# Values by seven products of half blocks, in turns with the keys, in an attention and graph convolution kernel

## The chip, the cores and the metric

The kernel runs on one core of a Trainium2 chip. Its time is the device time of one launch in microseconds (us); runs of one kernel on one chip are compared with runs of the other. In the profile, PE is TensorE, PEld its weight loads, DVE is VectorE, ACT is ScalarE, POOL is GpSimd, SP is the engine that issues the transfers. L405 is line 405 of the kernel.

## What is computed

The input is x, 16 batches of 1024 nodes with 256 channels, in fp32. Cut to what matters here, the first layer is

```python
fea  = transpose(x, (0, 2, 1))
Wg   = adj * likeness(mean of x over channels)      # per batch, 1024 x 1024
q    = relu((fea @ Wg) * para)                      # split in 4 heads of 64
kv   = x @ kv_w                                     # kv_w is 256 x 512
k, v = first 256 columns, last 256 columns          # keys and values, 4 heads each
out  = softmax(q k^T * scale) v
x    = layernorm(x + out)
```

The second layer is two graph convolutions with a residual and a layernorm:

```python
h = relu(x @ w1_loop + adj @ (x @ w1_neigh) + b1)
h = relu(h @ w2_loop + adj @ (h @ w2_neigh) + b2)
x = layernorm(x + (x + h) * 0.5)
```

The change concerns `v`, the values: per batch a product of x (1024 x 256) with the right half of `kv_w` (256 x 256).

## The kernel before

All 16 batches go through one long program whose order is written out by hand (`tc.manual_schedule()`): each engine does its instructions in the order in which the program names them, and waits where a tile isn't ready or its buffer isn't free. Work of several batches is woven together. While batch b is in its attention, the queries, keys and values of batch b + 1 are prepared, and the convolutions of batches b - 1 and b - 2 are done.

Attention of a batch has four units (two pairs of heads by two halves of the queries). A unit is `scores` (L594, TensorE, with the exponentials on ScalarE at L597 and their running sum on VectorE at L601 and L603) and then `outputs` (L614). After the fourth unit come the last products of the queries for the next batch (`FastQueries.step`, L546), then the keys and values of the next batch (`KeysValues.run`), and then the next batch's first scores, which need both.

Several products are already done by a scheme with seven products of half blocks in place of eight: the matrices are cut in 2 x 2 blocks, sums of blocks are made beforehand, and seven products are added up in a fixed pattern. The queries are done so (`FastQueries`, 28 products per batch, added by `end`, L555 to L563), the products with `adj` of the convolutions (`Joined`), and the keys (`KeysValues`). In `KeysValues`:

- `sums` makes the four sums of the blocks of x on VectorE; `self.w[n]` is the right factor of product n, [128 channels, 512 nodes].
- `sum_key_weights` makes the four sums of the key weights once, on GpSimd, and leaves them in DRAM; `load` brings them back for each batch (512 columns of a tile of 1024); `self.a[n]` is the left factor of product n, [128, 128].
- `run` does the products 1, 2, 6, 5, 7, 4, 3. Three products are added in PSUM onto an earlier one (`again=True`), after ScalarE has copied the earlier state out. Three PSUM tiles are used: 1, 6, 5 and 3 go to `first`; 2 to `third`; 7 and 4 to `second`.
- Between the keys' products stand four groups of the values. `value_group` (L355 to L362) makes two node tiles of 128 with all 256 channels: four products of 256 columns, with the tiles of x as weights.

A product of the program is two matmul instructions in the profile.

PSUM is shared out by two tags: `big`, three tiles of [128, 1024], and `bank`, two tiles of [128, 512]. `half_psum` takes a whole `big` tile and uses half of it. The tiles of a tag are handed out as they come free, and a tile is free when its last reader is done. The queries' products hold all three `big` tiles (products 1 and 6 in the first, 2 and 7 in the second, 5 and 3 in the third) and one `bank` tile (product 4) until `FastQueries.end` has added them up. Its adds read the first tile last at L556, the second at L558, the `bank` tile at L559 and the third at L563. Between L559 and L561 `end` calls `norm.sum_squares`, which sums the squares of the batch in normalization on VectorE (L319, L254).

`run` takes two callbacks. `between` is `norm.variance`: `fold_sums` (L247 to L251), one small product on TensorE that adds the sums of squares over the partitions, into a `bank` tile, and then the reciprocal deviation (L324 on VectorE, L326, a power, on GpSimd). `later` is `q.scale` (L569, L570), which finishes the queries. The part of the main loop that calls all this for batches 2 to 15:

```python
qT = q.end(norm.sum_squares)
xB = load_blocked(b + 1, f"a{b + 1}")
load_next()
kT, v = kv.run(norm.variance, q.scale)
...
norm.scale()
norm.spread()
```

Batches 0 and 1 use the plain functions `keys` and `values`.

Of the kernel before, what the change touches and what calls it, by code (L numbers as in the profile page):

```python
# [10 lines left out]
F32 = mybir.dt.float32  # L11
# [7 lines left out]
def kernel(  # L19
# [31 lines left out]
    nc = tc.nc  # L51

    B, N, C = x.shape
    P = 128
    NT = N // P
    NC = C // P
# [3 lines left out]
    FB = 512  # L60
    NJ = N // FB
    TJ = FB // P
    EPS = 1e-5
# [19 lines left out]
    dram = ctx.enter_context(tc.tile_pool(name="dram", bufs=2, space=bass.MemoryType.DRAM))  # L83

    def big_psum(name):
        return psum.tile([P, N], F32, tag="big", name=name, bufs=3)

    def half_psum(name):
        return big_psum(name)[:, 0:FB]

    def bank_psum(name):
        return psum.tile([P, FB], F32, tag="bank", name=name, bufs=2)
# [6 lines left out]
    def row_tile(name):  # L99
        return work.tile([P, N], F32, tag="row", name=name, bufs=ROWS)  # L100
# [15 lines left out]
    for t0 in range(0, NT, 2):  # L116
        nc.sync.dma_start(out=x_first[:, t0:t0 + 2, :],
                          in_=x[0, t0 * P:(t0 + 2) * P, :].rearrange("(t p) c -> p t c", p=P))
    kvw_sb = const.tile([P, NC, 2 * C], F32, name="kvw_sb")
# [6 lines left out]
    b2_sb = const.tile([P, C], F32, name="b2_sb")  # L126


    key_sums = dram.tile([P, 4 * P], F32, tag="key_sums", name="key_sums", bufs=1)

    def sum_key_weights():
        a11, a21, a12, a22 = (kvw_sb[:, cc, ts(kb, P)] for cc in range(NC) for kb in range(NC))
        t = row_tile("key_sums")
        s1, s2, s3, s4 = (t[:, ts(n, P)] for n in range(4))
        nc.gpsimd.tensor_add(s1, a21, a22)
        nc.gpsimd.tensor_sub(s2, s1, a11)
        nc.gpsimd.tensor_sub(s3, a11, a21)
        nc.gpsimd.tensor_sub(s4, a12, s2)
        nc.sync.dma_start(out=key_sums, in_=t[:, 0:4 * P])

    def load_weights():
        nc.sync.dma_start(out=w1l_sb, in_=w1_loop.rearrange("(cc p) f -> p cc f", p=P))
# [79 lines left out]
    def prepare_first(xb):  # L222

        xT = work.tile([P, NC, N], F32, tag="xT", name="xT_0", bufs=2)
        c_col = small.tile([P, NT], F32, tag="c_col", name="c_col_0", bufs=2)
        pts = [[half_psum(f"xT_ps_0_{cc}") for cc in range(NC)], [bank_psum(f"xT_ps_1_{cc}") for cc in range(NC)]]
        for j in range(NJ):
            for t in range(j * TJ, (j + 1) * TJ):
                for cc in range(NC):
                    nc.tensor.transpose(pts[j][cc][:, ts(t - j * TJ, P)], xb[:, t, ts(cc, P)], ident)  # L230
            for cc in range(NC):
                (nc.vector.tensor_copy if cc else nc.scalar.copy)(xT[:, cc, ts(j, FB)], pts[j][cc])
        for j in range(NJ):
            rows = slice(j * TJ, (j + 1) * TJ)
            nc.vector.tensor_reduce(c_col[:, rows], xb[:, rows, :], AX.X, ALU.add)
        nc.vector.tensor_scalar_mul(c_col, c_col, 1.0 / C)
        return xT, c_col
# [6 lines left out]
        nc.scalar.copy(c_row, pc)  # L244
        return c_row

    def fold_sums(part, name):  # L247

        pm = bank_psum(f"{name}_ps")
        nc.tensor.matmul(pm[:, 0:NB], fold.rearrange("p a k -> p (a k)"), part[:, 0, :], start=True, stop=True)  # L250
        return pm[:, 0:NB]  # L251

    def join(part):
        nc.vector.tensor_add(part[:, 0, :], part[:, 0, :], part[:, 1, :])  # L254
# [40 lines left out]
    def by_node(t):  # L295
        return t.rearrange("p (bn r) -> p bn r", r=S)

    class BlockedNorm:
# [22 lines left out]

        def variance(self):
            self.rstd = small.tile([P, NB], F32, tag="rstd1", name=f"rstd1_{self.name}", bufs=2)
            nc.vector.tensor_scalar(self.rstd, fold_sums(self.part, f"sum2_{self.name}"), 1.0 / C, EPS,  # L324
                                    op0=ALU.mult, op1=ALU.add)
            nc.gpsimd.tensor_tensor(self.rstd, self.rstd, neg_half, ALU.pow)  # L326

# [27 lines left out]
    def value_group(b, v, xT, g, copy):  # L355
        per = FB // C
        pv = bank_psum(f"v_ps_{b}_{g}")
        for i in range(per):
            for cc in range(NC):
                nc.tensor.matmul(pv[:, ts(i, C)], xT[:, cc, ts(g * per + i, P)], kvw_sb[:, cc, C:2 * C],  # L360
                                 start=(cc == 0), stop=(cc == NC - 1))
        copy(v[:, g * per:(g + 1) * per, :], pv.rearrange("p (i c) -> p i c", c=C))  # L362
# [7 lines left out]
    class KeysValues:  # L370
# [17 lines left out]
            self.w = {1: w11, 2: w21, 3: w22, 4: t4, 5: t1, 6: t2, 7: t3}  # L388

        def load(self):  # L390
            t = row_tile(f"key_sums_{self.b}")
            nc.sync.dma_start(out=t[:, 0:4 * P], in_=key_sums)
            a11, a21, a12, a22 = (kvw_sb[:, cc, ts(kb, P)] for cc in range(NC) for kb in range(NC))
            self.a = {1: a11, 2: a12, 3: t[:, ts(3, P)], 4: a22, 5: t[:, ts(0, P)], 6: t[:, ts(1, P)], 7: t[:, ts(2, P)]}

        def run(self, between, later):
            b, xT = self.b, self.xT
            kT = work.tile([P, NC, N], F32, tag="kT", name=f"kT_{b}")
            v = work.tile([P, NT, C], F32, tag="v", name=f"v_{b}")
            first, third, second = (half_psum(f"k_ps_{b}_{i}") for i in range(3))  # L400
            s12, s34 = (row_tile(f"ksnap_{b}_{k}") for k in range(2))
            p1, u1, u3, p7 = s12[:, 0:FB], s12[:, FB:N], s34[:, 0:FB], s34[:, FB:N]

            def product(n, dst, again=False):
                nc.tensor.matmul(dst, self.a[n], self.w[n], start=not again, stop=True, skip_group_check=again)  # L405

            def group(g):
                value_group(b, v, xT, g, nc.scalar.copy)

            product(1, first)  # L410
            nc.scalar.copy(p1, first)
            product(2, third)
            group(0)
            product(6, first, again=True)
            nc.scalar.copy(u1, first)
            group(1)
            between()
            nc.vector.tensor_add(kT[:, 0, 0:FB], p1, third)
            product(5, first, again=True)
            nc.scalar.copy(u3, first)  # L420
            product(7, second)
            nc.scalar.copy(p7, second)
            group(2)
            later()
            product(4, second, again=True)
            nc.vector.tensor_add(kT[:, 1, 0:FB], u1, second)
            nc.gpsimd.tensor_add(kT[:, 1, FB:N], u3, p7)
            product(3, first, again=True)
            nc.scalar.copy(kT[:, 0, FB:N], first)
            group(3)  # L430
            return kT, v

    class Queries:
# [49 lines left out]
    class FastQueries(Queries):  # L483
# [16 lines left out]
        def block(self, i, j):  # L500
            return self.xb[:, j * TJ:(j + 1) * TJ, ts(i, P)]
# [70 lines left out]
    class Attention:  # L572
# [47 lines left out]
        def add(self, u):  # L620

            b, (pair, j) = self.b, UNITS[u]
            half = FB // S
            pd = bank_psum(f"den_ps_{b}_{u}")
            den = pd[:, 0:2 * half]
            nc.tensor.matmul(den, fold.rearrange("p a k -> p (a k)"), self.part.pop(u), start=True, stop=True)  # L626
            rden = self.rden[:, ts(u, half)]
            for s in range(2):
                rows = slice(s * HD, (s + 1) * HD)
                nc.vector.reciprocal(rden[rows, :], den[rows, ts(s, half)])  # L630
            o = by_node(self.o.pop(u))
            nc.vector.tensor_mul(o, o, rden.unsqueeze(2).to_broadcast([P, half, S]))
            dst = by_node(self.xB[pair][:, ts(j, FB)])
            nc.vector.tensor_add(dst, dst, o)
            nc.vector.tensor_reduce(self.sums[:, pair, ts(j, half)], dst, AX.X, ALU.add)
            if u == len(UNITS) - 1:
                join(self.sums)
                nc.vector.tensor_reduce(rden_min[:, b:b + 1], self.rden, AX.X, ALU.min)
                nc.vector.tensor_reduce(rden_max[:, b:b + 1], self.rden, AX.X, ALU.max)
# [274 lines left out]
    def run():  # L914
# [10 lines left out]
        xT, c_col = prepare_first(x_first)  # L925
        q = Queries(0, x_first)
        for t in range(NT):
            q.load(t)
        sum_key_weights()
        q.load_para()  # L930
        blocked = load_blocked(1, "1")
        tiles = {mt: adj_blocked(mt) for mt in (0, TJ, 1)}
# [6 lines left out]
        kT = keys(0, xT, first_weights)  # L939
        for t in (1, 2):  # L940
            q.likeness(t)
        v = values(0, xT, nc.vector.tensor_copy)
# [28 lines left out]
        for b in range(B):  # L971
# [87 lines left out]
            if more and not c1:  # L1059
                xT = ready["xT"]  # L1060
# [32 lines left out]
                kT, v = keys(b + 1, xT), values(b + 1, xT)  # L1093
            elif more:
# [11 lines left out]
                kT, v = kv.run(norm.variance, q.scale)  # L1106
# [33 lines left out]
    with tc.manual_schedule():  # L1140
        run()
# [14 lines left out]
    with tc.If(count < P):  # L1156
        with tc.For_i(0, B, 1) as b:
            xb = load_x(b, "z")
            xT = channel_major(load_blocked(b, "z"), "xT_z")
            q = Queries("z", xb)  # L1160
            means(q, xb, "z")()
            kT, v = keys("z", xT), values("z", xT)
# [46 lines left out]
```

## Time and profile before

| | |
|---|---|
| time, median of 3 runs | 2170.1 us (2170.02 to 2170.28) |
| span of the profiled run | 2168.3 us |
| granted TensorE clock, mean | 0.999 |
| busy: TensorE, VectorE, ScalarE, GpSimd | 2153.5, 1892.3, 1027.7, 367.2 us |
| values, L360, all batches, TensorE busy | 120.2 us |
| keys in `KeysValues`, L405, 196 instructions | 96.7 us |

The first lines are for the whole program; the busy time of an engine counts the time in which at least one of its instructions runs. The last two rows are the groups of instructions of those lines; the 96.7 is the sum of the four groups of L405 (41.8, 26.3, 14.3 and 14.3 us). Matmuls overlap one another, so the distance from one start to the next says what a product costs, and not the length of one record.

### The profile page before, as it was taken

How to read it: one execution, taken by the hardware profiler on the slowest of the kernel's cores; microseconds unless marked ns; L12 is line 12 of the kernel's file. 1: busy time of each engine (PE TensorE's matmuls, PEld its weight loads, DVE VectorE, ACT ScalarE, POOL GpSimd, SP SyncE). 2: the span in 40 equal slices, each digit the busy share in tenths (PEclk: the TensorE clock that was granted, in tenths of full speed). 3: DMA queues.
4: the chain of work that ended last, by engine and by line, in shares of the span. 5: the costliest groups of instructions: out<-in, count | busy, mean ns of one | idle time of the engine just before them, and what ended most of it. 6: DMA issues, size and time to landing. Idle time of an engine off the chain costs nothing.

```text
span 2168.3 us, 23079 instructions
## 1 busy us (share of the span) xinstructions
PE 2153.5 (99%) x8054; PEld 1024.9 (47%) x8054; DVE 1892.3 (87%) x2343; ACT 1027.7 (47%) x1346; POOL 367.2 (17%) x208
## 2 busy tenths in 40 slices
PE   9999999999999999999999999999999999999997
PEld 5344444444444444444544445454454444544354
DVE  5978998898998989988889888999989899898965
ACT  4744545545355453445444454445553445535411
POOL 1011130211303113030120302203022130211021
PEclk9999999999999999999999999999999999999999
DMA  9493663846557375573655536566384654744342
GB/s 230 117 136 117 139 158 101 143 130 117 147 127 161 102 127 154 128 171 89 115 165 124 160 88 116 171 122 156 97 123 154 122 155 115 131 137 83 117 138 97
DMA packets 611771, 286.22 MB, mean 132 GB/s; under 512 B 504768, under 2 KB 569152, under 8 KB 611648
## 3 DMA queue, kind: packets, MB, share of 16 engines
q1 hardware_dynamic: 611376, 284.15, 55.5%
q8 instruction: 65, 1.06, 0.2%
q14 instruction: 58, 0.48, 0.1%
q10 hardware_dynamic: 272, 0.52, 0.1%
HBM read 238.16 MB, written 46.46 MB: 131 GB/s over the span
## 4 chain that ended last, share of the span: by engine, by line
PE 97%; DVE 2%; ACT 0%; DMA 0%; issue 0%; SPq 0%; POOLq 0%; DVEq 0%; POOL 0%
PE s L594 20%; PE av L614 20%; PE hu_ps L873 17%; PE g_ps L546 16%; PE v_ps L360 5%; PE k_ps L405 4%; PE t_ps L712 3%; PE h_ps L780 3%; PE hu_ps L719 2%; PE g_ps L473 2%; PE h_ps L781 2%; DVE acc L603 1%; PE h_ps L734 1%; PE u_ps L763 1%; PE k_ps L350 1%; PE den_ps L626 0%
## 5 line engine op out<-in xcount | busy, mean ns | idle before, releaser
L597 ACT ACTIVATE pr<-s 128x1024 f32<-128x1024 f32 x512 | 476.1, 1052 | 176.6 <-PE s L594 176.6
L603 DVE TENSOR_TENSOR acc<-acc,pr 128x1024 f32<-128x1024 f32 x384 | 494.1, 1287 | 41.1 <-DVE acc L603 1.0
L594 PE MATMUL s<-qT,kT 64*128 64x512 f32 x2048 | 457.1, 596 | 0.7 <-ACT qT L480 0.7
L614 PE MATMUL av<-pr,v 128*64 128x512 f32 x2048 | 453.6, 595 | 0.0
L594 PEld LDWEIGHTS s<-qT,kT 64*128 64x128 f32 x2048 | 191.1, 185 | 236.1 <-ACT pr L597 114.1
L614 PEld LDWEIGHTS av<-pr,v 128*64 128x64 f32 x2048 | 141.4, 137 | 300.0 <-issue 285.7
L326 POOL TENSOR_TENSOR rstd<-rstd,neg_half 128x32 f32<-128x32 f32 x16 | 87.1, 5443 | 1111.5 <-DVE rstd L324 1111.5
L459 ACT ACTIVATE wg<-c_row,c_col 128x1024 f32<-128x1024 f32 x128 | 146.9, 1148 | 69.5 <-DVE accB L605 51.3
L465 DVE SCALAR_TENSOR_TENSOR wg<-wg,adj 128x1024 f32<-128x1024 f32 x128 | 149.8, 1209 | 11.3 <-ACT wg L460 10.4
L873 PE MATMUL hu_ps<-adj,R 128*128 128x512 f32 x360 | 158.3, 596 | 0.0
L460 ACT ACTIVATE wg<-wg 128x1024 f32<-128x1024 f32 x128 | 135.3, 1057 | 4.1
L314 ACT ACTIVATE sq<-xB_a 128x1024 f32<-128x1024 f32 x32 | 33.8, 1057 | 194.4 <-DVE xB_a L309 193.1
L360 PE MATMUL v_ps<-kvw_sb,xT 128*128 128x256 f32 x512 | 120.2, 379 | 0.1
L546 PE MATMUL g_ps<-wg,S 128*128 128x512 f32 x224 | 116.7, 603 | 0.0
L360 PEld LDWEIGHTS v_ps<-kvw_sb,xT 128*128 128x128 f32 x512 | 97.2, 190 | 38.4 <-issue 21.0
L546 PE MATMUL g_ps<-T,S 128*128 128x512 f32 x224 | 114.4, 592 | 0.0
L546 PE MATMUL g_ps<-wg,x 128*128 128x512 f32 x224 | 109.0, 599 | 0.0
L873 PE MATMUL hu_ps<-adjT,t 128*128 128x512 f32 x240 | 105.7, 592 | 0.0
L873 PEld LDWEIGHTS hu_ps<-adj,R 128*128 128x128 f32 x360 | 67.3, 190 | 78.9 <-issue 78.4
L601 DVE TENSOR_TENSOR acc<-pr,pr 128x1024 f32<-128x1024 f32 x64 | 76.8, 1200 | 23.7 <-ACT pr L597 23.7
L605 DVE STREAM_TRANSPOSE accB<-acc 128x1024 f32<-128x1024 f32 x64 | 79.7, 1245 | 3.2
L889 ACT COPY snap<-hu_ps 128x512 f32<-128x512 f32 x15 | 8.8, 586 | 150.2 <-PE hu_ps L873 150.2
(185 smaller groups left out, 2916.0 us busy)
## 6 DMA issues: line engine op xcount, KB each, us to landing
adj<-in_adj_dram SPq DMA_DIRECT2D x128, 512.0 KB, 4.5
adj<-adjT SPq DMA_DIRECT2D x120, 512.0 KB, 10.2
para<-in_L_gnn_para_dram SPq DMA_DIRECT2D x32, 512.0 KB, 3.3
xB_a<-in_x_dram SPq DMA_DIRECT2D x128, 128.0 KB, 4.2
x1d<-xB_a SPq DMA_DIRECT2D x128, 128.0 KB, 3.4
x<-x1d SPq DMA_DIRECT2D x16, 1024.0 KB, 15.4
xB<-in_x_dram SPq DMA_DIRECT2D x120, 128.0 KB, 4.5
x<-in_x_dram SPq DMA_DIRECT2D x15, 1024.0 KB, 7.0
```

The costliest lines, as they stand in the source:

```text
L326: nc.gpsimd.tensor_tensor(self.rstd, self.rstd, neg_half, ALU.pow)
L360: nc.tensor.matmul(pv[:, ts(i, C)], xT[:, cc, ts(g * per + i, P)], kvw_sb[:, cc, C:2 * C], start=(cc == 0), stop=(cc == NC - 1))
L405: nc.tensor.matmul(dst, self.a[n], self.w[n], start=not again, stop=True, skip_group_check=again)
L459: nc.scalar.activation(wg, self.c_row, AF.Abs, bias=self.c_col[:, t:t + 1], scale=-1.0)
L460: nc.scalar.activation(wg, wg, AF.Tanh, scale=-0.5)
L465: nc.vector.scalar_tensor_tensor(wg, wg, 1.0, self.adj.pop(t), op0=ALU.add, op1=ALU.mult)
L546: nc.tensor.matmul(self.p[n], x_n[:, k, :], w_n, start=(k == 0), stop=(k == TJ - 1))
L594: nc.tensor.matmul(ps[:, ts(s, FB)], self.kT[rows, pair, ts(mt, P)], self.qT[rows, pair, ts(j, FB)], start=True, stop=True)
L597: nc.scalar.activation(pr, ps, AF.Exp)
L603: nc.vector.tensor_add(acc, acc, pr)
L614: nc.tensor.matmul(pav[s * HD:(s + 1) * HD, :], self.v[:, mt, pair * P + s * HD:pair * P + (s + 1) * HD], self.pr[mt][:, ts(s, FB)], start ...
L873: nc.tensor.matmul(dst, self.x[n][:, k, :], half_adj[w][:, k, :] if w else of_rows(rows, k), start=(start and k == 0), stop=(k == TJ - 1), ...
```

## The change

The values are now computed by seven products of half blocks too. Their right factors are cut from the other half of `kv_w`, with sums made once at the start as for the keys (`sum_kv_weights`, now a full tile of 1024 columns); the sums of x are those of the keys, used here as weights. A value product n is four matmuls of 128 columns, one for each node tile of the half. Keys and values take turns: key n, value n, in the order 1, 2, 6, 7, 5, 4, 3. The purpose is less work on TensorE: 28 products of 128 columns in place of 16 of 256 columns.

The value products hold two `bank` tiles (`v_first` for products 1, 6, 5 and 3, `v_next` for 2 and then for 7 and 4). The fold of the variance therefore goes to a `big` tile. It stands after key 2 and value 2; before, it stood after key 2, group 0, key 6 and group 1.

```diff
-    def sum_key_weights():
+    def sum_kv_weights():
+        t = row_tile("kv_sums")
+        for k in range(2):
+            a11, a21, a12, a22 = (kvw_sb[:, cc, ts(2 * k + kb, P)] for cc in range(NC) for kb in range(NC))
+            s1, s2, s3, s4 = (t[:, ts(4 * k + n, P)] for n in range(4))
...
+        nc.sync.dma_start(out=kv_sums, in_=t)
...
-    def fold_sums(part, name):
+    def fold_sums(part, name, psum_tile=bank_psum):
-        pm = bank_psum(f"{name}_ps")
+        pm = psum_tile(f"{name}_ps")
...
-            nc.vector.tensor_scalar(self.rstd, fold_sums(self.part, f"sum2_{self.name}"), 1.0 / C, EPS,
+            nc.vector.tensor_scalar(self.rstd, fold_sums(self.part, f"sum2_{self.name}", half_psum), 1.0 / C, EPS,
...
+        def value(self, n, dst, again=False):
+            for t in range(TJ):
+                nc.tensor.matmul(dst[:, ts(t, P)], self.w[n][:, ts(t, P)], self.a[1][n],
+                                 start=not again and t == 0, stop=True, skip_group_check=again or t > 0)
...
-            product(1, first)
-            nc.scalar.copy(p1, first)
-            product(2, third)
-            group(0)
-            product(6, first, again=True)
-            nc.scalar.copy(u1, first)
-            group(1)
+            k_first, v_first = half_psum(f"k_ps_{b}_0"), bank_psum(f"v_ps_{b}_0")
+            self.key(1, k_first)
+            copy(p1, k_first)
+            self.value(1, v_first)
+            copy(y1, v_first)
+            k_next, v_next = half_psum(f"k_ps_{b}_1"), bank_psum(f"v_ps_{b}_1")
+            self.key(2, k_next)
+            self.value(2, v_next)
             between()
-            nc.vector.tensor_add(kT[:, 0, 0:FB], p1, third)
-            product(5, first, again=True)
-            nc.scalar.copy(u3, first)
-            product(7, second)
-            nc.scalar.copy(p7, second)
-            group(2)
+            add(kT[:, 0, 0:FB], p1, k_next)
+            add(block(0, 0), tiles(y1), tiles(v_next))
+            self.key(6, k_first, again=True)
+            copy(u1, k_first)
+            self.value(6, v_first, again=True)
+            copy(z1, v_first)
+            k_next, v_next = half_psum(f"k_ps_{b}_2"), bank_psum(f"v_ps_{b}_2")
+            self.key(7, k_next)
+            copy(p7, k_next)
+            self.value(7, v_next)
+            copy(y7, v_next)
+            self.key(5, k_first, again=True)
+            copy(u3, k_first)
+            self.value(5, v_first, again=True)
+            copy(z3, v_first)
             later()
-            product(4, second, again=True)
-            nc.vector.tensor_add(kT[:, 1, 0:FB], u1, second)
+            self.key(4, k_next, again=True)
+            add(kT[:, 1, 0:FB], u1, k_next)
             nc.gpsimd.tensor_add(kT[:, 1, FB:N], u3, p7)
-            product(3, first, again=True)
-            nc.scalar.copy(kT[:, 0, FB:N], first)
-            group(3)
+            self.value(4, v_next, again=True)
+            self.key(3, k_first, again=True)
+            copy(kT[:, 0, FB:N], k_first)
+            add(block(1, 0), tiles(z1), tiles(v_next))
+            self.value(3, v_first, again=True)
+            copy(block(0, 1), tiles(v_first))
+            nc.gpsimd.tensor_add(block(1, 1), tiles(z3), tiles(y7))
             return kT, v
```

`block(i, j)` is the half of the value tile with channels i and node tiles j; `y1`, `z1`, `z3` and `y7` are ScalarE's copies of the value products, in two more row tiles.

## The prediction

> **What bounds the kernel now.** I read the page first, then the groups of instructions with the shapes kept apart, then the waits of TensorE, and last the timeline of one batch's keys and values. Of the page, the first block gives busy time and share of the span of each engine, the second the engines' shares of the chain that ended last:
>
> ```profile
> PE 2153.5 (99%) x8054; PEld 1024.9 (47%) x8054; DVE 1892.3 (87%) x2343; ACT 1027.7 (47%) x1346; POOL 367.2 (17%) x208
> ...
> PE 97%; DVE 2%; ACT 0%; DMA 0%; issue 0%; SPq 0%; POOLq 0%; DVEq 0%; POOL 0%
> ```
>
> TensorE is the bound, and the list of its waits adds up to about 4 us over the whole span. So there is no slack on TensorE to hide anything in: a microsecond less of its work is a microsecond gained, and a microsecond in which it waits is one lost. VectorE at 87% is the engine to suspect for such waits.
>
> What a product costs comes from the groups by form. After the x stand the number of instructions, the busy time of the group, and the mean length of one; each product of the program is two instructions here:
>
> ```profile
> L360 PE MATMUL v_ps<-kvw_sb,xT 128*128 128x256 f32 x512 | 120.2, 379 | 0.1
> ...
> L712 PE MATMUL t_ps<-w1n_sb,x1T 128*128 128x128 f32 x512 | 61.3, 278 | 0.0
> ```
>
> The mean lengths overlap one another and are not what counts; the distance from start to start does. It can be read in the timeline (start, length, engine, line, operation, number of instructions merged) of batch 8's keys and values, which run while batch 7 is normalized:
>
> ```profile
> 1054.40 1.88 PE L405 MATMUL k_ps<-xT,kvw_sb 128*128 128x512 f32 x4
> 1056.12 1.89 PE L360 MATMUL v_ps<-kvw_sb,xT 128*128 128x256 f32 x8
> 1057.85 1.02 PE L405 MATMUL k_ps<-K,key_sums 128*128 128x512 f32 x2
> 1058.70 1.89 PE L360 MATMUL v_ps<-kvw_sb,xT 128*128 128x256 f32 x8
> 1060.43 0.30 PE L250 MATMUL sum_ps<-sq_part,fold 128*128 128x32 f32 x2
> 1060.57 1.96 PE L405 MATMUL k_ps<-K,key_sums 128*128 128x512 f32 x4
> ...
> 1067.63 7.14 PE L594 MATMUL s<-qT,kT 64*128 64x512 f32 x32
> ```
>
> and, from the same view of VectorE,
>
> ```profile
> 1053.22 0.69 DVE L556 TENSOR_TENSOR U<-P,g_ps 128x512 f32<-128x512 f32 x1 [1.66 <-ACT P L555]
> 1053.82 0.68 DVE L557 TENSOR_TENSOR qT<-P,g_ps 128x512 f32<-128x512 f32 x1
> 1054.42 0.68 DVE L558 TENSOR_TENSOR U<-U,g_ps 128x512 f32<-128x512 f32 x1
> 1055.20 0.69 DVE L559 TENSOR_TENSOR qT<-U,g_ps 128x512 f32<-128x512 f32 x1
> 1055.81 2.34 DVE L319 TENSOR_REDUCE sq_part<-sq 128x32 f32<-128x1024 f32 x2
> 1058.18 0.19 DVE L254 TENSOR_TENSOR sq_part<-sq_part 128x32 f32<-128x32 f32 x1
> 1058.29 0.68 DVE L561 TENSOR_TENSOR qT<-U,g_ps 128x512 f32<-128x512 f32 x1
> 1058.89 0.68 DVE L562 TENSOR_TENSOR U<-U,g_ps 128x512 f32<-128x512 f32 x1
> 1059.60 0.69 DVE L563 TENSOR_TENSOR qT<-U,g_ps 128x512 f32<-128x512 f32 x1
> ```
>
> Call the start of the first key product T0 (1054.40). The stage ends when the scores start, T0 + 13.23. A key product takes (1056.12 - 1054.40)/2 = 0.86 us, a value group of four products of 256 columns 1.73, the fold (L250, the sum over channels of the squares) 0.14. Seven keys, four groups and the fold make 6.02 + 6.92 + 0.14 = 13.08; the stage has no hole. Look at where VectorE stands: it adds up the queries' seven products (L556 to L559), sums the squares in between (L319, L254), and finishes the queries with L561 to L563, whose last ends at 1060.29, T0 + 5.89. The fold starts at T0 + 6.03, just after.
>
> [...]L712, with 128 columns and a new weight each time, needs 3.67 us for 16 products, 0.229 each, against 0.433/2 = 0.216 for the same columns in L360. [...]
>
> **The change part by part.** It touches 14 of the 16 batches (L405 has 196 instructions: 14 x 7 x 2).
>
> *Products.* Removed per batch: 16 products of 256 columns, 4 x 1.73 = 6.92 us. Added: 7 x 4 = 28 products of 128 columns. The form is that of L712 (weights 128x128, 128 columns moving), so 28 x 0.229 = 6.42. Bounds: [...]0.38 if two unhidden weight loads of 190 ns set the pace; L712 excludes the latter unless the order matters. I take 0.229. Gain 0.50 us per batch, 14 x 0.50 = 7.0 in all.
>
> *Order on TensorE, and the fold.* Before, the fold comes after keys 1, 2, 6 and two value groups (3 x 0.86 + 2 x 1.73 = 6.03 after T0, as measured). After, it comes after keys 1 and 2 and values 1 and 2: 2 x 0.858 + 8 x 0.229 = 3.55. It thus arrives 2.5 us earlier. It needs the sum of squares, which L254 gives at 1058.37, T0 + 3.97: a wait of 0.4 at least.
>
> *Buffers.* The fold's PSUM tile moves from `bank` (two) to `big` (three), because the two `bank` tiles are now held by the value products until after the fold. What of `big` is free then? The three held the queries' products: the pair (1, 6), the pair (2, 7), the pair (5, 3). The first key tile takes the first (free after L556), the second takes the second (free after L558), and both are still live. Only the third is left, and L563 is its last reader. In the built order the fold's one wait is on VectorE, at that add. So it can start at T0 + 5.89, plus about 0.05 for the signal (the end of the kernel shows one such: the copy L775 ends at 2153.79, TensorE resumes at 2153.84). TensorE arrives at 3.55 and starts at 5.94: idle for 2.39 us. Behind the fold in TensorE's queue stand all the other ten products; VectorE's rstd, both first adds and GpSimd's power wait for it too.
>
> Is L563 still at T0 + 5.89? VectorE has no gap from L785 in the scores of the last unit (1015.70) up to L556, where it waits for ScalarE's copy, itself behind two squares. All that keeps its order relative to TensorE, and nothing in it is edited. I leave 5.89.
>
> *After the fold.* Fold with its exposed load 0.24 (0.14, and 0.1 by which the restart at 2153.84 is longer than its neighbours). Then five keys and five values, 5 x 0.858 + 5 x 0.918 = 8.88, and the same 0.09 before the scores: T0 + 5.94 + 0.24 + 8.88 + 0.09 = 15.15, against 13.23. That is +1.92 us per batch, 14 x 1.92 = +26.9.
>
> *Copies and adds.* ScalarE has ten copies of 0.59 in place of nine; each product that adds onto a PSUM tile starts 2.6 us or more after the end of the one before it on that tile, against 0.2 + 0.59 for the copy, so none holds TensorE. ScalarE is tight only at the end: two activations for the queries (1.0 each) and the last key copy end some 0.15 before the scores; I take nothing, 0.1 per batch at most. VectorE has two more adds of 0.69, one behind the other in front of the normalization's scaling; this puts its lag behind the scores from 4.5 us to 4.9, and the denominators of the first unit (ready 16.2 after the scores' start, wanted at 17.8) still come in time. GpSimd has one more add of 1.27 after the power; the block is not read until the third unit's outputs. All nothing.
>
> *Transfers.* The sums of the weights are 512 KB in place of 256, loaded 14 times, issued 17 us before they are read (1040.64 against 1057.85): hidden. Four more GpSimd operations of 0.46 at the start lie in a 34 us gap of that engine.
>
> Sum: 2170.1 + 26.9 = 2197.0.
>
> **The rivals.** (1) The fold finds its buffer free and TensorE never waits: then only the 7.0 count, 2163.1. For it: no wait of TensorE in the loop reached a microsecond before. Against it: three buffers, two live, and the time of L563 in the trace. (2) VectorE gets ahead, because TensorE's later stage gives it time, and L563 ends a microsecond earlier: 14 x (1.92 - 1) = 13, 2183. Against it: VectorE waited for ScalarE's copy and, at 1015.70, for TensorE itself, so it is already as early as these let it. (3) The narrow products cost their weight loads, 0.38: arrival at 1.72 + 3.04 = 4.76, still a wait up to 5.94, then 0.24 + 4.29 + 20 x 0.38 + 0.09, the end at 18.2; 14 x 4.9 = 69, 2239. Against it: L712.
>
> **How the numbers follow.** Forecast 0.86, rival (1) 0.06, (2) 0.05, (3) 0.03. Within the forecast, the restart can cost 0.1 more or less, the narrow products after the fold 0.3 less to 0.2 more per batch, the last copy 0.1: about -6 to +6 us. Taken out to near rival (2) on the low side, and a little for waits not seen on the other: 2187 to 2205, which holds some 0.84. Faster 0.06 (rival 1), slower 0.92; 0.02 for a wait that just eats the gain.
>
> **What would show it.** In the profile after: TensorE idle before the fold's line, 14 times, about 2.4 us each and 33 in all, released by the last add of the queries; narrow value products at 0.229 from start to start; the scores 15.1 us after the first key product; no other wait of TensorE above 0.1. I am wrong if the fold starts less than 5 us after T0, if the wait is put down to the sum of squares alone, or if another product in the stage waits.

## The result and the profile after

| | before | after |
|---|---|---|
| time, median | 2170.2 us | 2216.4 us (2214.6 to 2221.2, 5 runs) |
| ratio to before, 95% interval | | 1.0218 (1.0207 to 1.0229) |
| span of the profiled run | 2168.3 us | 2219.3 us |
| mean granted TensorE clock | 0.999 | 0.987 |

The change makes the kernel 46.2 us slower. The forecast was 26.9 us slower, with a range up to 2205. The direction and the wait were foreseen; a cost that follows the wait was not. It shows in the last row of the table: part of the time TensorE did not have its full clock. The profiled run is the slowest of the five (2221.2 us).

The page of the profile after begins like that of before, but the chain that ended last now runs over VectorE for a seventh of the span:

```profile
PE 2172.6 (98%) x8390; PEld 1048.0 (47%) x8390; DVE 1894.5 (85%) x2371; ACT 1037.5 (47%) x1360; POOL 384.3 (17%) x226
...
PE 83%; DVE 14%; ACT 1%; issue 1%; DMA 0%; SPq 0%; ACTq 0%; DVEq 0%; POOLq 0%; POOL 0%
```

TensorE's waits (line that waits, what ended the wait, us in total, times, longest) have one new entry at the head. The others, of which the first is shown, are there before the change too and reach 1.4 us at most:

```profile
PE sum_ps L251 <- DVE qT L593: 32.1, 14, 2.6
PE idle L954 <- POOL ident masks.py:199: 1.4, 1, 1.4
```

L251 is the fold, L593 the last add of the queries (L250 and L563 before). It is the wait of the forecast: 14 times, 32.1 us against the 33 named there. Now the same stage as in the prediction, the keys and values of batch 8 in TensorE's timeline:

```profile
1077.06 1.02 PE L401 MATMUL k_ps<-xT,kvw_sb 128*128 128x512 f32 x2
1077.92 1.05 PE L405 MATMUL v_ps<-kvw_sb,xT 128*128 128x128 f32 x8
1078.81 1.02 PE L401 MATMUL k_ps<-xT,kvw_sb 128*128 128x512 f32 x2
1079.67 1.05 PE L405 MATMUL v_ps<-kvw_sb,xT 128*128 128x128 f32 x8
1082.99 0.41 PE L251 MATMUL sum_ps<-sq_part,fold 128*128 128x32 f32 x2 [2.26 <-DVE qT L593]
1083.23 1.12 PE L401 MATMUL k_ps<-K,kv_sums 128*128 128x512 f32 x2
1084.17 1.89 PE L405 MATMUL v_ps<-kv_sums,K 128*128 128x128 f32 x8
1085.86 1.89 PE L401 MATMUL k_ps<-K,kv_sums 128*128 128x512 f32 x2
1087.57 1.07 PE L405 MATMUL v_ps<-kv_sums,K 128*128 128x128 f32 x8
1088.48 1.02 PE L401 MATMUL k_ps<-K,kv_sums 128*128 128x512 f32 x2
1089.34 1.05 PE L405 MATMUL v_ps<-kv_sums,K 128*128 128x128 f32 x8
1090.23 1.02 PE L401 MATMUL k_ps<-K,kvw_sb 128*128 128x512 f32 x2
...
1093.83 1.56 PE L624 MATMUL s<-qT,kT 64*128 64x512 f32 x6
```

and VectorE's last add of the queries, which the fold waits for:

```profile
1082.25 0.69 DVE L593 TENSOR_TENSOR qT<-U,g_ps 128x512 f32<-128x512 f32 x1
```

Up to the fold all goes by the forecast: it starts 5.93 us after the first key product (5.94 forecast). A value product takes 1078.81 - 1077.92 = 0.89 us, a little less than the 0.92 taken. Then look at value 6 and key 7, which start at 1084.17 and 1085.86: they take 1.69 and 1.71 us, twice what the same forms take a few lines further on (0.89 from 1089.34, 0.86 from 1088.48), and neither shows a wait, so nothing that the timeline shows holds them up. From the scores at 1093.83 to the next batch's first key product (1213.80) it is 119.97 us, just as before the change (1067.63 to 1187.60): the loss is made in this stage, which lasts 16.77 us in place of 13.23. The reason stands in the view of stretches of 1 us (busy time of the five engines, then the granted clock, the share of the transfers, and GB/s):

```profile
1082.00:1083.00 1.00, 0.01 (x1) 0.01 (x1) 0.90 (x2) 0.00 (x0) 0.00 (x0) 1.00 1.30 162
1083.00:1084.00 1.00, 1.00 (x4) 0.70 (x5) 0.57 (x2) 0.00 (x0) 0.30 (x1) 1.00 1.39 152
1084.00:1085.00 1.00, 1.00 (x5) 0.82 (x4) 1.00 (x3) 0.59 (x1) 1.00 (x1) 0.59 1.16 104
1085.00:1086.00 1.00, 1.00 (x6) 1.00 (x6) 1.00 (x2) 0.00 (x0) 1.00 (x1) 0.50 0.01 0
1086.00:1087.00 1.00, 1.00 (x3) 0.48 (x2) 1.00 (x1) 0.59 (x1) 1.00 (x1) 0.50 0.00 0
1087.00:1088.00 1.00, 1.00 (x5) 0.48 (x5) 0.09 (x1) 0.21 (x1) 1.00 (x1) 0.70 0.00 0
1088.00:1089.00 1.00, 1.00 (x8) 0.76 (x8) 0.00 (x0) 0.70 (x2) 1.00 (x1) 1.00 0.00 0
```

TensorE counts as fully busy here, but from 1084.2 to 1087.6 it has half its clock (0.50). On the page this can't be seen: its row of forty slices shows the clock as 9 in every slice, for a slice is 55 us long.

### The profile page after: what moved, and what is told of

It is laid out like the page before. It is cut to its first block, busy times and chain, and to the rows that moved or that the text cites. A ratio compares the mean times of both kernels' runs of the same rounds, so it can differ in the third digit from the quotient of the medians.

```text
span 2219.3 us, 23826 instructions
## 1 busy us (share of the span) xinstructions
PE 2172.6 (98%) x8390; PEld 1048.0 (47%) x8390; DVE 1894.5 (85%) x2371; ACT 1037.5 (47%) x1360; POOL 384.3 (17%) x226
## 4 chain that ended last, share of the span: by engine, by line
PE 83%; DVE 14%; ACT 1%; issue 1%; DMA 0%; SPq 0%; ACTq 0%; DVEq 0%; POOLq 0%; POOL 0%
PE s L624 20%; PE av L644 20%; PE hu_ps L903 16%; PE g_ps L576 4%; PE k_ps L401 3%; PE v_ps L405 3%; PE t_ps L742 3%; DVE wg L495 3%; PE h_ps L810 2%; PE hu_ps L749 2%; PE g_ps L503 2%; PE h_ps L811 2%; DVE sq_part L320 1%; DVE T L551 1%; DVE wg L549 1%
## 5 line engine op out<-in xcount | busy, mean ns | idle before, releaser
L327 POOL TENSOR_TENSOR rstd<-rstd,neg_half 128x32 f32<-128x32 f32 x16 | 87.1, 5441 | 1112.7 <-DVE rstd L325 1112.7
L637 DVE TENSOR_REDUCE den_part<-accB 128x32 f32<-128x1024 f32 x64 | 78.1, 1220 | 2.2
L810 PE MATMUL h_ps<-w2n_sb,uT 128*128 128x256 f32 x240 | 72.7, 385 | 0.0
```

The source lines that it names most:

```text
L810: nc.tensor.matmul(p2[:, ts(i, C)], self.uT[:, ts(t, P)], w2n_sb, start=True, stop=False)
```

## The experiments

Two theories stood after the result. The *clock theory*: the wait itself lowers the clock for a while. The *crowding theory*: what the fold releases at once (two adds out of PSUM, GpSimd's power, the copies) slows TensorE, and the clock row shows something else. A third question was whether the wait comes from the buffer, as forecast, or from the sum of squares or VectorE's queue.

### Filling the wait

The change is kept, and useless key products are put ahead of the fold. Edit (three runs, with n = 3, 1 and 2):

```diff
-            k_next, v_next = half_psum(f"k_ps_{b}_1"), bank_psum(f"v_ps_{b}_1")
+            k_pair, v_next = big_psum(f"k_ps_{b}_1"), bank_psum(f"v_ps_{b}_1")
+            k_next = k_pair[:, 0:FB]
             self.key(2, k_next)
             self.value(2, v_next)
+            for _ in range(n):
+                self.key(2, k_pair[:, FB:N])
             between()
```

> The changed kernel with three more key products (key 2 again, into the unused half of its PSUM tile; nothing reads them) ahead of the fold, so that TensorE works through the 2.3 us in which it waited. Clock theory (the wait itself sets TensorE to half clock for some 3.4 us, which costs 1.65 us per batch beside the wait): no wait, no half clock, scores at 3.5 + 2.57 + 0.14 + 8.74 + 0.09 = 15.04 us after the first key product, 14 x 1.81 above before, about 2195. Crowding theory (what is released together after the fold, two adds out of PSUM, GpSimd's power and the copies, slows the products): as slow as without the filling, 2216 to 2219.

> The same with one extra product: the wait shrinks from 2.3 us to about 1.5. Clock theory: if 1.5 us of idle time is too little to lower the clock, scores at 15.0 us, about 2195; if it is enough, 2216 as without filling; something between if it happens in some batches only. Crowding theory: 2216.

> The same with two extra products: the wait shrinks to about 0.6 us. Clock theory: no lowered clock, about 2195. Crowding theory: 2216.

| extra products | wait at the fold, sum of 14 | time | ratio to before |
|---|---|---|---|
| 0 (the change) | 32.1 us | 2216.4 us | 1.0218 (1.0207 to 1.0229) |
| 1 | 20.0 us | 2197.8 us | 1.0128 (1.0111 to 1.0145) |
| 2 | 8.0 us | 2197.0 us | 1.0124 (1.0107 to 1.0141) |
| 3 | none | 2197.3 us | 1.0125 (1.0109 to 1.0142) |

More work makes the kernel 19 us faster. All three fillings give nearly the same time: with one and two the fold still starts at the end of the queries' last add (L596 in these kernels), with three the filling ends 0.15 us later, and what follows the fold keeps its full clock (the mean of each of the three profiled runs is 0.998, in runs of the kernel before 0.998 to 0.999). TensorE's timeline with one extra product:

```profile
1069.60 1.02 PE L401 MATMUL k_ps<-xT,kvw_sb 128*128 128x512 f32 x2
1072.03 0.41 PE L251 MATMUL sum_ps<-sq_part,fold 128*128 128x32 f32 x2 [1.41 <-DVE qT L596]
1072.27 1.10 PE L401 MATMUL k_ps<-K,kv_sums 128*128 128x512 f32 x2
1073.21 1.05 PE L405 MATMUL v_ps<-kv_sums,K 128*128 128x128 f32 x8
1074.10 1.02 PE L401 MATMUL k_ps<-K,kv_sums 128*128 128x512 f32 x2
1074.96 1.05 PE L405 MATMUL v_ps<-kv_sums,K 128*128 128x128 f32 x8
```

Value 6 and key 7 take 0.89 and 0.86 with the same releases behind the fold as in the change. The crowding theory falls. The 27.1 us that are left with three fillings are what the forecast made of the later fold (26.9); the other 19.1 are the clock. The 19.1 hold for the median of the change. Its profiled run stands 23.8 us over the filled kernel, with 15 stretches of 3.41 us at half clock, or 1.6 us each. The fastest of the five is 17.3 us over, which by the same reckoning makes some 11. That is an estimate, for of that run only the mean clock was recorded: 0.990, against 0.987 in the profiled run.

### A wait between 1.4 and 2.3 us

One extra product of 256 columns in place of 512:

```diff
+            nc.tensor.matmul(k_pair[:, FB:FB + 2 * P], self.a[0][2], self.w[2][:, 0:2 * P], start=True, stop=True)
             between()
```

> The changed kernel with one extra product of 256 columns (half of key 2 again, read by nothing) ahead of the fold: the wait is about 1.9 us, between 1.4, which left the clock alone, and 2.3, which lowered it in every batch looked at. If the length of the idle time within some fixed stretch decides, some or all batches keep their clock: between 2197 and 2216, and near 2197 if the bound lies above 1.9. If any wait of TensorE over 1.5 us does it, 2216.

Measured: 2216.3 us, ratio 1.0213 (1.0198 to 1.0229), with 26.0 us of waits in 14, 1.86 each. So the filling gained nothing over the change here. In the profiled run the clock was lowered to 0.50 after 11 of the 14 waits and left alone after 3, though the waits are nearly alike.

### The same wait in the kernel before

No narrow products, no moved fold: only key product 7 moved up, to where its tile isn't free yet.

```diff
             product(2, third)
             group(0)
+            product(7, second)
+            nc.scalar.copy(p7, second)
             product(6, first, again=True)
             nc.scalar.copy(u1, first)
             group(1)
             between()
...
             nc.scalar.copy(u3, first)
-            product(7, second)
-            nc.scalar.copy(p7, second)
             group(2)
```

> The kernel before with its values untouched, and only key product 7 moved up behind the first value group, where its tile is not free yet: a wait of about 2.5 us on TensorE for the same add of the queries, with no narrow products and with the fold in its old tile. Clock theory: the wait costs 2.5 us and some 1.65 more at half clock, 14 x 4.2, about 2228. Theory that the slow stretch belongs to the new products (their weights from the row tile, or the fold's release): the wait alone, 14 x 2.5, about 2205.

Measured: 2216.3 us, ratio 1.0215 (1.0200 to 1.0231), between the two theories' numbers. The trace says why: the wait is there 14 times (32.5 us), and the clock fell to 0.50 after 5 of them. Two such waits in TensorE's timeline, one with the clock lowered and one without:

```profile
941.54 3.60 PE L405 MATMUL k_ps<-K,key_sums 128*128 128x512 f32 x4 [2.33 <-DVE qT L563]
944.98 1.89 PE L360 MATMUL v_ps<-kvw_sb,xT 128*128 128x256 f32 x8
```

```profile
1078.96 1.98 PE L405 MATMUL k_ps<-K,key_sums 128*128 128x512 f32 x4 [2.33 <-DVE qT L563]
1080.78 1.89 PE L360 MATMUL v_ps<-kvw_sb,xT 128*128 128x256 f32 x8
```

The same two products after the same wait of 2.33 us take 3.44 us from start to start once and 1.82 the other time. The new products are therefore not needed for the loss; a wait is. What decides between the two cases follows below, under what was not expected.

### The fold in a tile that is free

The fold goes into the unused half of the second key product's tile:

```diff
-            between()
+            between(lambda name: k_pair[:, FB:N])
```

with `variance` taking the tile's giver as an argument.

> The changed kernel with the fold in the unused half of the second key product's PSUM tile, so that it waits for the sum of squares alone and no longer for the queries' last add. Buffer theory (that the wait was for a free tile): the fold starts 4.0 us after the first key product, a wait of 0.5 us, scores at 4.02 + 0.24 + 8.74 + 0.09 = 13.1 against 13.23, 2168. If the sum of squares or VectorE's queue was the cause: 2216. If the slow products come from what is released after the fold and not from the wait: 14 x 1.65 above the first number, 2191.

Measured: 2177.0 us, ratio 1.0031 (1.0020 to 1.0043). TensorE's waits at the head of its list:

```profile
PE k_ps L251 <- DVE sq_part L255: 5.2, 14, 0.7
PE v_ps L405 <- DVE v L437: 2.8, 14, 0.2
PE den_ps L657 <- DVE den_part L638: 1.9, 2, 1.1
```

The fold now waits for the sum of squares only, 0.4 us each time, and starts 1062.04 - 1058.03 = 4.01 us after the first key product. The buffer was the cause of the long wait. The time is 9 us over the forecast of this run mostly because of the second line: with the first wait shortened, value 7 comes to its `bank` tile before VectorE's add of value 2 (L437) has read it.

```profile
1058.03 1.02 PE L401 MATMUL k_ps<-xT,kvw_sb 128*128 128x512 f32 x2
...
1062.04 0.41 PE L251 MATMUL k_ps<-sq_part,fold 128*128 128x32 f32 x2 [0.35 <-DVE sq_part L255]
...
1064.12 1.02 PE L401 MATMUL k_ps<-K,kv_sums 128*128 128x512 f32 x2
1065.34 1.13 PE L405 MATMUL v_ps<-kv_sums,K 128*128 128x128 f32 x8 [0.20 <-DVE v L437]
1066.31 1.02 PE L401 MATMUL k_ps<-K,kv_sums 128*128 128x512 f32 x2
```

Key 7 and value 7 take 2.19 us from start to start (1064.12 to 1066.31), where 0.86 + 0.89 = 1.75 would do. That is 0.44 per batch, more than the 0.20 of idle time shows, and 6.2 us in all; where the rest comes from stays open. From the first key product to the scores it is 13.63 us, 0.40 more than before.

### A version that is faster

The fold's place is changed too: behind product 6 of keys and values, with products 5 ahead of 7, so that TensorE has work until the sum, the tile and VectorE's adds are there.

```diff
             self.key(2, k_next)
             self.value(2, v_next)
-            between(lambda name: k_pair[:, FB:N])
-            add(kT[:, 0, 0:FB], p1, k_next)
-            add(block(0, 0), tiles(y1), tiles(v_next))
             self.key(6, k_first, again=True)
             copy(u1, k_first)
             self.value(6, v_first, again=True)
             copy(z1, v_first)
+            between(lambda name: k_pair[:, FB:N])
+            add(kT[:, 0, 0:FB], p1, k_next)
+            add(block(0, 0), tiles(y1), tiles(v_next))
+            self.key(5, k_first, again=True)
+            copy(u3, k_first)
+            self.value(5, v_first, again=True)
+            copy(z3, v_first)
             k_next, v_next = half_psum(f"k_ps_{b}_2"), bank_psum(f"v_ps_{b}_2")
             self.key(7, k_next)
             copy(p7, k_next)
             self.value(7, v_next)
             copy(y7, v_next)
-            self.key(5, k_first, again=True)
-            copy(u3, k_first)
-            self.value(5, v_first, again=True)
-            copy(z3, v_first)
```

> The fold in the unused half of the second key product's tile as in the run before, and moved behind products 6; products 5 ahead of 7. If all that stood against the change was the place of the fold and its buffer, TensorE works through: 7 x 0.858 + 7 x 0.89 + 0.14 + 0.09 = 12.47 us from the first key product to the scores, 0.76 less than before, 14 x 0.76 = 10.7, about 2160. If the narrow products or the turns cost something else, for instance a wait for the copies or the adds between them, it ends between 2165 and 2177.

Measured: 2172.6 us, ratio 1.0008 (1.0000 to 1.0016): a miss by 13 us. In the stage TensorE no longer waits: 1070.05 - 1057.39 = 12.66 us to the scores, 0.57 less than before and 0.19 more than worked out. But a wait has come up elsewhere, in front of the first unit's denominators (L657), 14 times and 6.2 us in all. It eats the gain: from the scores to the next first key product it is 120.51 us (1070.05 to 1190.56), 0.54 more than before. VectorE is late there; its scaling of the normalization (L332) and GpSimd's work in the same microseconds show why:

```profile
1069.08 4.34 DVE L332 TENSOR_TENSOR xB_a<-xB_a,rstd 128x1024 f32<-128x1024 f32 x2
...
1063.45 5.44 POOL L327 TENSOR_TENSOR rstd<-rstd,neg_half 128x32 f32<-128x32 f32 x1 [70.58 <-DVE rstd L325]
1068.86 1.27 POOL L454 TENSOR_TENSOR kT<-ksnap 128x512 f32<-128x512 f32 x1
1070.09 2.25 POOL L461 TENSOR_TENSOR v<-vsnap 128x512 f32<-128x512 f32 x1
```

Two scalings take 4.34 us where the kernel before has 3.42, and the new add on GpSimd 2.25. They meet because both come after GpSimd's power (L327, done at 1068.89): the scaling needs its result, and the adds stand behind it in GpSimd's order. In batch 2 the wait for the denominators is 1.97 us long and the clock falls once: its mean from 270 to 300 us is 0.94, and 1.00 in the stretches on either side.

In the next two runs GpSimd's adds go to VectorE, both, or the values' alone:

```diff
             later()
+            add(kT[:, 1, FB:N], u3, p7)
             self.key(4, k_next, again=True)
             add(kT[:, 1, 0:FB], u1, k_next)
-            nc.gpsimd.tensor_add(kT[:, 1, FB:N], u3, p7)
+            add(block(1, 1), tiles(z3), tiles(y7))
...
-            nc.gpsimd.tensor_add(block(1, 1), tiles(z3), tiles(y7))
```

> The mended order of the run before last but one, with the two adds of GpSimd (last block of the keys, last block of the values) on VectorE, where they take 0.69 each. In that run the stage was 0.57 us shorter than before, but VectorE's scaling of the normalization took 4.3 us in place of 3.4 while GpSimd's two adds ran, and the first denominators came late. Theory that the two engines slow each other: the scaling takes 2.4 us, the denominators come in time, and the 14 x 0.57 = 8 us show: 2162. Theory that VectorE's plain load is the limit: 1.4 us more of it per batch makes the denominators later still, 2175 or more.

> The same with only the values' add on VectorE and the keys' add left on GpSimd as in the kernel before. If the engines slow each other, the scaling takes some 3.4 us as in the kernel before, and the time lies between 2162 and 2172. If plain load is the limit, 2174 or so.

Measured: 2162.1 us, ratio 0.9963 (0.9949 to 0.9976), with both; 2163.0 us, ratio 0.9966 (0.9954 to 0.9978), with the values' alone. These are the fastest of the study, 8 us under before. From the page of the run before these two (first line) and of the one with both adds moved (second), the first row:

```profile
PE 2150.4 (99%) x8390; PEld 1031.5 (48%) x8390; DVE 1940.1 (89%) x2371; ACT 1037.9 (48%) x1360; POOL 399.4 (18%) x226
```

```profile
PE 2145.4 (99%) x8390; PEld 1029.8 (48%) x8390; DVE 1908.0 (88%) x2399; ACT 1037.6 (48%) x1360; POOL 351.1 (16%) x198
```

VectorE has 28 instructions more and is busy 32 us less. The scaling of batch 8 takes 2.35 us with both adds moved, 3.06 with one, and TensorE's wait for denominators is back at 0.8 us in all with both. Here two adds of 0.69 us per batch, moved to an engine that was busy for 18% of the span, had cost VectorE more than they took off.

## Why the prediction was right and wrong

- *The products.* Right in kind, the size a little off: 0.89 us per value product against 0.918. Seven per batch make 0.20 us, 2.7 us in all, in the change's favour. The best version shows the gain as real: its stage is 0.57 us shorter than before, which is 8.0 us in 14 batches, and it is 8.1 us faster.
- *The fold comes early and waits for its tile.* Right, step by step: arrival, start (5.93 for 5.94), releaser (L593), sum (32.1 for 33), and by the run with another tile the cause. The products behind the fold stand still with it, as taken: in batch 8 TensorE runs nothing from the end of value 2 (1080.72) to the fold (1082.99), and key 6 follows at 1083.23.
- *"VectorE's chain is not moved."* Right: L593 ends 5.88 us after the first key product, 5.89 before.
- *After the fold.* Here it failed. The step was "five keys and five values, 5 x 0.858 + 5 x 0.918 = 8.88", which prices each product as it runs at full clock, and behind it the sentence that a microsecond in which TensorE waits is one lost; it was more than one. In batch 8 these ten take 10.51 us (1083.23 to 0.09 ahead of 1093.83). The term left out is the clock lost behind a wait, some 1.7 us where it falls (half of 3.41); over the launch 19.1 us (2216.4 less the 2197.3 with the wait filled). The other 27.1 of the 46.2 us are the forecast's own sum: with one extra product, where the wait is there and the clock stays, the stage lasts 15.10 us (1066.10 to 1081.20), for 15.15 forecast. That it fits so closely is in part luck: the five values behind the fold are 0.14 us cheaper than taken, and key 6, at 0.94 us right behind the fold, is 0.08 dearer.
- *Copies, adds, transfers taken at nothing.* Right for the change: no other wait of the stage is in its list. In the faster orders, where TensorE doesn't wait, two of them turned out to be worth something: the second add in front of value 7 (0.2 us of wait in the run with its own half) and GpSimd's add (the whole gain).
- *The rivals.* None came true. The range's upper end, 8 us over the forecast (6 for its own terms and "a little for waits not seen"), had no room for a second cost of the wait itself. The trace of before could not show it, for TensorE has no wait over 1.4 us in it. What the runs show of it, a clock of 0.50 for 3.41 us behind 2.05 us of wait, stands in the last section.

## What to carry to other kernels

When TensorE is the bound, price a new wait twice: its own length, and a stretch at half clock behind it if it is long (here 3.41 us of it, 1.7 us lost, behind waits of some 2 us), and ask of any change that brings products forward what they will find when they arrive (a tile, a sum). Read the granted clock in stretches of a microsecond around a wait, since a slice of the page averages it away (0.987 was the mean of the whole run), and take products of double length with no wait as its sign (1.69 us for 0.89). If a wait can't be taken away, fill it with products nobody reads: here that took 19 us off.

## What was not expected of the hardware

*The clock falls on a grid of its own.* In stretches of 0.1 us each lowered stretch behind a wait is 3.41 us long at a clock of 0.50, or twice that in one case. Two neighbours in the change start 136.53 us apart (1084.19 and 1220.72), 40 times 3.4133, while their folds start 136.73 apart (1082.99 and 1219.72). In each run the starts of all of them leave the same remainder on division by 3.4133 us: 2.16 in the change (14 stretches after 14 waits, one of them twice as long), 0.78 in the run with half a product (11), 2.74 in the run with the wait in the kernel before (5). So in these runs the lowered stretches lie on a grid that doesn't follow the program. Call one step of it a window, and count the part of a wait that lies in the window ahead of each grid point. In the kernel before with the wait, where full-length products stand on both sides of it, a window with 2.05 us of the wait in it was followed by half clock and one with 1.98 us was not. The other waits of that run sort in the same way: four more windows held 2.20 us or more and were followed by half clock, and the eight waits that a border cut into parts of at most 1.81 us were not, which fits the 5 of 14. With one extra product the waits were 1.43 us on average and 1.8 at most, and the mean clock stayed at 0.998. In the run with 1.83 us the wait alone does not sort the cases; with the 0.24 us of the fold behind it counted as idle too, it does (2.07 and more, lowered; 1.94 cut by the border, not). The one lowered stretch of the later order can be placed by the weight loads of the scores, which stand 0.85 us apart from 289.25 to 291.81 and 0.43 before and after: it starts near 289.1. By an estimate from these, some 1.75 us of the wait for the denominators lie in the 3.41 us ahead of it, and the denominators' own narrow products take 0.34 more (287.44 to 287.78). That narrow products count as idle is the author's inference from these cases and was not tried by itself. One case stays open: the stretch of two windows in the change (from 807.71), whose first window had only the last 0.30 us of a wait and the fold in it.

*VectorE and GpSimd slow each other.* In batch 8 two scalings (L332) took 2.35 us with no add on GpSimd, 3.06 with the keys' add there and 4.34 beside both, and a GpSimd add that takes 1.27 took 2.25. Not all of GpSimd's work does this: beside its power in the same batch of the later order, two multiplications of the same size (L600) took 2.35 us (1064.48 to 1066.83). One after the other, the scalings and the two adds would take 2.35 + 2 x 1.27 = 4.89 us, by an estimate from these lengths; side by side they took 4.56 (1068.86 to 1073.42). Why the two slow each other was not shown.
